# A graph-attention kernel with a larger ring of gathered tiles, smaller ALU layers, and extra TensorE products

## The chip, the cores and the metric

The kernel runs on one core of one Trainium2 chip. The metric is the device time of one execution in microseconds (us), the median of several runs. The profiles were taken from single executions of the same program.

## The reference

6250 nodes of 512 features and 100000 edges, sorted by their destination. First a layer of attention over the graph, then a small feed-forward "ALU" that reads a few features of each node. Cut to what matters:

```python
xn = layernorm(x)                                   # (6250, 512)
q, k, v = xn @ Wq + bq, xn @ Wk + bk, xn @ Wv + bv  # 8 heads of 64
logits = (q[rows] / 8 * k[cols]).sum(-1) + edge_attr          # (100000, 8)
att = segment_softmax(logits, rows)
y = segment_sum(att * v[cols], rows)
x = x + y @ Wo + bo
z = layernorm(x)
# ALU: 16-way decodes of z give four digits; two pipelines (add, sub)
# of three 160x160 layers with relu, on two positions of a node
out = x + z
out[:, 128:161] += one_hot(results), carry          # for active nodes
```

## The kernel before

**Two stages.** The first (0 to about 660 us of the span) sorts the edges on VectorE and, beside that, computes layer norm, K and V of all nodes on TensorE and writes them to DRAM as a table kv_d of 6250 rows of 1024 numbers (K and V side by side). The main stage follows: 49 blocks of 128 nodes (one node per partition). A block has a fixed number of edge slots, from 34 down to 8 (CAP), 804 in all; block b is cut into parts of at most 12 slots.

**A part.** Two slots share a tile kvt of [128, 2, 1024] float32 (8 KB in each partition), from a pool kvp of 11 buffers, the ring. For each slot GpSimd issues an indirect DMA (`gather`, L110) that fetches 128 rows of kv_d. It also fetches, some blocks ahead, the edges' records (rec), keys (kg) and node rows (xg), all in one queue in program order. The part is then worked on like this:

- `dots`: VectorE multiplies K by q in place (L814) and sums over each head (L815). So after L814 the K half of the tile holds the products k*q.
- `softmax`: VectorE takes the maximum and subtracts it, ScalarE takes the exponential (L752) and copies the weights into the PSUM tile pp (L756). pp has 256 columns, two halves used in turn.
- `sums`, called after the first dots of the next part (the list `waiting`): VectorE sums the weights (L767), VectorE multiplies the V half of most tiles by the weights in pp (L825), ScalarE does so for the last one or two full tiles (L823), and TensorE adds all slots up into the PSUM tile p_y by matmuls with the identity (L1105). The last of these matmuls on a tile frees it for the ring.
- `part_end`, a generator: VectorE adds p_y to y (L1064, L1068), divides (L790); `attend_out` transposes y on TensorE (L833), ScalarE copies it (L836), TensorE multiplies it by Wo (L842), VectorE adds x (L846).
- `project` (a generator too) makes q of the next block: transposes of xg (L803), a ScalarE copy (L805), the product with Wq (L809).

A float32 matmul of 512 columns stands in the trace as two passes.

**The ALU.** Four blocks form a group (the last are smaller). `alu` is a generator over the whole group's 512 nodes: TK = 512 nodes are taken at once through a first layer (L906, five matmuls, relu by ScalarE at L908 into h1), a second (L919, relu at L921 into h2) and a third (L926, copied by VectorE to yf at L929). All of them use the PSUM tag "mm", which has two buffers. The generator yields a kind ("P", "E" or "D") for the next step.

**Order.** All engines run in the order in which the program is written (`manual_schedule`). `pump(kinds)`, called once per tile before its `dots`, moves every generator in `going` one step, and the ALU one step if its kind is in `kinds` (`alu_steps`); at the end of a part up to four "P" steps are taken. So each engine has one fixed queue, in which a waiting instruction holds up all behind it.

SBUF holds, beside the ring, h1 and h2 (10 KB in each partition each), yf and fT (2 KB each in eight partitions), x1 and others.

Of the kernel before, what the change touches and what calls it, by code (L numbers as in the profile page):

```python
# [10 lines left out]
F32 = mybir.dt.float32  # L11
I32 = mybir.dt.int32
BF16 = mybir.dt.bfloat16
AF = mybir.ActivationFunctionType
# [6 lines left out]
P = 128  # L21
# [5 lines left out]
LOM = (1 << LOB) - 1  # L27
ROW = 9
GB = 4
TK = 512  # L30
LA = 6


# [10 lines left out]
def gnn_ffn_kernel(  # L44
# [3 lines left out]
    nc = tc.nc  # L48
    N, D = x.shape
    E = src.shape[0]  # L50
    H = edge_attr.shape[1]
# [22 lines left out]
    def ctile(shape, name, dt=F32, pool=const):  # L74
        return pool.tile(shape, dt, tag=name, name=name)
# [33 lines left out]
    def gather(dst_t, table, idx):  # L109
        nc.gpsimd.indirect_dma_start(  # L110
            out=dst_t, out_offset=None, in_=table,
            in_offset=bass.IndirectOffsetOnAxis(ap=idx, axis=0))
# [4 lines left out]
    wq = ctile([P, KC, D], "wq", pool=ow)  # L117
# [17 lines left out]
    NC4 = 4  # L135
# [87 lines left out]
    def fetch_keys(b):  # L223
        C = CAP[ORDER[b]]
        t, nbuf = ("0", 1) if b == 0 else ("", LA + 3)
        kg = pre.tile([P, C + 1], F32, tag="kg" + t, name="kg", bufs=nbuf)
        gather(kg, words, pos_i[:, ORDER[b]:ORDER[b] + 1])
        st[b] = dict(kg=kg)
# [18 lines left out]
    def fetch_recs(n, last):  # L247

        while fetched[0] < n and fetched[1] is not None and fetched[1][0] <= last:
            b, s = fetched[1]  # L250
            gather(st[b]["rec"][:, s, :], rec_d, st[b]["eid"][:, s:s + 1])
            fetched[:] = fetched[0] + 1, next(wanted, None)
# [5 lines left out]
    with tc.tile_pool(name="sort", bufs=1, side="right") as sp, \  # L258
# [75 lines left out]
        def zeros(shape, name):  # L334
            t = ctile(shape, name, pool=ow)
            nc.gpsimd.memset(t, 0.0)
            return t

        w0 = zeros([8, (NC4 + 1) * P], "w0")
        w2 = zeros([P, NC4 + 1, 2 * NC4], "w2")  # L340
# [388 lines left out]

    main = dict(reuse_waits="tile")  # L730
    ap_ = ctx.enter_context(tc.tile_pool(name="ap", bufs=2, **main))
    kvp = ctx.enter_context(tc.tile_pool(name="kvp", bufs=11, **main))
    o2 = ctx.enter_context(tc.tile_pool(name="o2", bufs=1, **main))
    ops = ctx.enter_context(tc.tile_pool(name="ops", bufs=2, space=PSUM, **main))

    turn_ = [0, 0]
    assert CG * H <= P
    pp = ops.tile([P, 2 * P], F32, tag="pp", name="pp", bufs=1)

    def softmax(lg, rec, m0):  # L740

# [57 lines left out]
    def project(xg, s_):  # L799

        pt = ops.tile([P, KC, P], F32, tag="tr", name="tr", bufs=1)
        for c in range(KC):
            nc.tensor.transpose(pt[:, c, :], xg[:, D + c * P:D + (c + 1) * P], ident)  # L803
        xT = o2.tile([P, KC, P], F32, tag="xT", name="xT", bufs=2)
        nc.scalar.copy(xT, pt)  # L805
        yield
        q = s_["q"] = ops.tile([P, D], F32, tag="q", name="q")
        for c in range(KC):
            nc.tensor.matmul(q, xT[:, c, :], wq[:, c, :], start=(c == 0), stop=False)  # L809
        nc.tensor.matmul(q, ones3, bq3, start=False, stop=True)  # L810

    def dots(kvt, n, q, dot, s):
        k = kvt[:, :n, :D]
        nc.vector.tensor_tensor(k, k, q[:, None, :].to_broadcast([P, n, D]), op=OP.mult)  # L814
        nc.vector.tensor_reduce(  # L815
            dot[:, s:s + n, :], k.rearrange("p s (h d) -> p s h d", h=H), AX.X, OP.add)
# [34 lines left out]
    def alu(x1, mv, n):  # L851
# [43 lines left out]
        fT = o2.tile([8, GB * P], F32, tag="fT", name="fT")  # L895
        nc.vector.tensor_copy(fT[:, :ntok], pf[:8, :ntok])  # L896


        yf = o2.tile([8, GB * P], F32, tag="yf", name="yf")
        for t0 in range(0, ntok, TK):  # L900
            t1 = min(t0 + TK, ntok)
            nt = t1 - t0
            h1 = o2.tile([P, NC4 + 1, TK], F32, tag="h1", name="h1")
            for c in range(NC4 + 1):
                pm = ops.tile([P, D], F32, tag="mm", name="pm3")
                nc.tensor.matmul(pm[:, :nt], w0[:, c * P:(c + 1) * P], fT[:, t0:t1],  # L906
                                 start=True, stop=True)
                nc.scalar.activation(h1[:, c, :nt], pm[:, :nt], AF.Relu,  # L908
                                     bias=b0[:, c:c + 1], scale=1.0)
                yield "P"  # L910
            h2 = o2.tile([P, NC4 + 1, TK], F32, tag="h2", name="h2")
            for c in range(NC4 + 1):
                if c < NC4:
                    terms = [(w1mm[c // 2], c), (w1lm[c], NC4)]
                else:
                    terms = [(w1ml[k], k) for k in range(NC4)] + [(w1ll, NC4)]
                pm = ops.tile([P, D], F32, tag="mm", name="pm4")
                for i, (w, k) in enumerate(terms):
                    nc.tensor.matmul(pm[:, :nt], w, h1[:, k, :nt],  # L919
                                     start=(i == 0), stop=(i == len(terms) - 1))  # L920
                nc.scalar.activation(h2[:, c, :nt], pm[:, :nt], AF.Relu,  # L921
                                     bias=b1[:, c:c + 1], scale=1.0)
                yield "P"
            p3 = ops.tile([P, D], F32, tag="mm", name="p3")[:8]
            for c in range(NC4 + 1):
                nc.tensor.matmul(p3[:, :nt], w2[:, c, :], h2[:, c, :nt],  # L926
                                 start=(c == 0), stop=(c == NC4))
            yield "D"
            nc.vector.tensor_copy(yf[:, t0:t1], p3[:, :nt])  # L929
# [51 lines left out]
    def fetch_nodes(b):  # L981
        if b - 4 in ends:
            run(ends.pop(b - 4))
        xg = ap_.tile([P, 2 * D], F32, tag="xg", name="xg", bufs=4)
        gather(xg, xx_d, nid[:, b:b + 1])
        st[b]["xg"] = xg
# [10 lines left out]
    kind = ["P"]  # L997
# [6 lines left out]
    def pump(kinds="", n=1):  # L1004

        last[1] += 1
        for g in list(going):
            if next(g, True):
                if g in going:
                    going.remove(g)  # L1010
        alu_steps(kinds, n)
        if stores and stores[0][0] + last[0] <= last[1]:
            store()

    def alu_steps(kinds, n):

        while alus and n > 0 and kind[0] in kinds:
            kind[0] = next(alus[0], None)
            if kind[0] is None:
                alus.pop(0)  # L1020
                kind[0] = "P"
            n -= 1

    def run(g):

# [87 lines left out]
    for b in range(NB):  # L1113
        C = CAP[ORDER[b]]
        s_ = st[b]
        rec, q = s_["rec"], s_["q"]
        parts = -(-C // PART)
        m = None
        for i in range(parts):
            s0, s1 = C * i // parts, C * (i + 1) // parts  # L1120
            n_ = s1 - s0
            dot = ap_.tile([P, n_, H], F32, tag="dot", name="dot", bufs=2)
            kvs = []
            for s in range(s0, s1, 2):
                n = min(2, s1 - s)
                kvt = kvp.tile([P, 2, 2 * D], F32, tag="kv", name="kv")
                for j in range(n):
                    gather(kvt[:, j, :], kv_d, rec[:, s + j, 0:1].bitcast(I32))
                kvs.append((kvt, n, s - s0))
                done = sum(SLOTS[:b]) + s + n  # L1130
                if done > HOLD:
                    last[0] = 1000
                fetch_recs(FIRST + (TOTAL - FIRST) * done // (TOTAL - LAST), b + LA)
                if s == s0 and i == 0:
                    if b + LA + 2 < NB:
                        fetch_keys(b + LA + 2)
                    if b + 1 < NB:
                        fetch_nodes(b + 1)
                if s == s0 + 2 and i == 0 and b + 1 < NB:
                    pj = project(st[b + 1]["xg"], st[b + 1])  # L1140
                    going.insert(0, pj)


                k = len(kvs) - 1
                pump("" if k < 2 else "D" if s + 2 >= s1 else "DE" if k == 2 else "DEP")
                dots(kvt, n, q, dot, s - s0)
                if s == s0:
                    for f in waiting:
                        f()
                    waiting.clear()  # L1150
                if s == s0 + 2 and i == parts - 1 and b + LA + 2 < NB:
                    read_keys(b + LA + 2)
            m, cor, p_ps = softmax(dot, rec[:, s0:s1], m)
            waiting.append(partial(sums, b, i, parts, dot, cor, p_ps, kvs, n_))
            alu_steps("P", min(4, len(kvs) - 1))
        if b + 1 < NB:
            run(pj)
# [150 lines left out]
```

## Time and profile before

| | |
|---|---|
| median of 14 runs | 3276.85 us (3251.86 to 3310.4) |
| the profiled execution, time | 3249.39 us |
| its span | 3247.6 us |
| mean granted TensorE clock | 0.801 |
| TensorE busy in the span | 2062.2 us (64%) |
| VectorE busy | 2004.7 us (62%) |
| ScalarE busy | 880.9 us (27%) |
| GpSimd busy | 1708.6 us (53%) |
| in the main stage, 660 to 3123 us: TensorE, VectorE, ScalarE, GpSimd busy | 1540, 1662, 638, 1504 us |
| granted clock, share of the DMA engines in it | 0.79, 0.57 |

How to read it: PE is TensorE, PEld its weight loads, DVE VectorE, ACT ScalarE, POOL GpSimd. A group's row gives the line, the engine, the operation, what it writes and reads, the count, then busy us and mean ns of one, then the idle time of the engine just before them and what ended most of it. The ends of matmuls are modelled. "issue" is a wait that the profile shows no cause for; "remote" and "an unknown queue" are waits whose end it cannot name. GpSimd's gathers take about 0.95 us each and are 0.30 us apart at the closest, and that gap is not counted as busy.

### The profile page before, as it was taken

The page shows a single profiled execution, that of the slowest core. Times are in us where ns is not written, and L with a number is a line of the kernel's source. Part 1 is how long each engine was busy: PE and PEld are TensorE (multiplying, and loading weights), DVE is VectorE, ACT ScalarE, POOL GpSimd, SP SyncE. Part 2 cuts the span into 40 slices and gives each one's busy share as a digit, 9 for nine tenths or more (in the row PEclk, how much of TensorE's full clock was granted, in tenths as well). Part 3 has the DMA queues.
Part 4 walks back from the last instruction along what each step waited for, and adds up shares of the span by engine and source line. Part 5 has one row for each costly group of instructions (what it writes and reads, how often), then busy time and mean ns, then how long its engine had stood idle before and what let it go on. Part 6 is the DMA issues. An engine that isn't in the chain of part 4 may idle for free. (4 is left out here: it accounts for less than half of the span.)

```text
span 3247.6 us, 20109 instructions
## 1 busy us (share of the span) xinstructions
PE 2062.2 (64%) x4853; PEld 889.9 (27%) x4853; DVE 2004.7 (62%) x3502; ACT 880.9 (27%) x2656; POOL 1708.6 (53%) x1860
## 2 busy tenths in 40 slices
PE   7887318743647645657476676757646748467686
PEld 3443103311212222222232232323222323123233
DVE  9887000075747655666686668768576756676772
ACT  6443003121113212222132222323213223122332
POOL 2010770165666565556655666666576555656630
PEclk9999658866868877878778888888877878788797
DMA  8443113366545455555655656665566555646630
GB/s 271 172 154 114 30 17 124 133 211 211 177 151 196 150 188 163 172 168 190 204 171 179 196 185 200 196 201 182 165 209 195 167 179 173 192 151 204 206 117 17
DMA packets 193964, 542.30 MB, mean 167 GB/s; under 512 B 51831, under 2 KB 53174, under 8 KB 193841
## 3 DMA queue, kind: packets, MB, share of 16 engines
q0 software_dynamic: 154416, 464.27, 44.9%
q1 hardware_dynamic: 39425, 76.67, 6.7%
q8 instruction: 42, 0.69, 0.1%
q14 instruction: 81, 0.66, 0.1%
HBM read 472.60 MB, written 68.22 MB: 167 GB/s over the span
## 5 line engine op out<-in xcount | busy, mean ns | idle before, releaser
L110 POOL DMA_INDIRECT kv<-kv_d,rec x804 | 760.4, 946 | 734.6 <-PE p_y L1105 300.8
L1105 PE MATMUL p_y<-kv,ident 128*128 128x512 f32 x1608 | 830.9, 673 | 351.2 <-issue 141.5
L110 POOL DMA_INDIRECT rec<-rec_d,eid x804 | 763.6, 950 | 245.1 <-issue 237.2
L814 DVE TENSOR_TENSOR kv<-kv,q 128x1024 f32<-128x1024 f32 (+1 forms) x425 | 490.2, 1153 | 199.1 <-DMA kv<-kv_d,rec 123.2
L1105 PEld LDWEIGHTS p_y<-kv,ident 128*128 128x128 f32 x1608 | 337.5, 216 | 819.1 <-issue 532.4
L815 DVE TENSOR_REDUCE dot<-kv 128x16 f32<-128x1024 f32 (+1 forms) x425 | 493.9, 1162 | 65.3 <-ACT kv L823 31.0
L809 PE MATMUL q<-wq,xT 128*128 128x512 f32 x392 | 212.9, 693 | 296.8 <-issue 203.9
L823 ACT ACTIVATE kv<-kv,dot 128x64 f32<-128x64 f32 x1568 | 387.3, 336 | 33.2 <-issue 32.2
L825 DVE TENSOR_TENSOR kv<-kv,pp 128x1024 f32<-128x1024 f32 (+1 forms) x327 | 352.7, 1137 | 0.0
L842 PE MATMUL pm<-wo,yT 128*128 128x512 f32 x392 | 215.4, 701 | 187.9 <-issue 101.4
L467 PE MATMUL pm<-wv,xnT 128*128 128x512 f32 (+1 forms) x392 | 190.2, 621 | 17.6 <-issue 17.6
L805 ACT COPY xT<-tr 128x512 f32<-128x512 f32 x49 | 28.7, 585 | 619.6 <-remote 328.6
L809 PEld LDWEIGHTS q<-wq,xT 128*128 128x128 f32 x392 | 82.6, 222 | 398.2 <-issue 301.4
L467 PE MATMUL pm<-wk,xnT 128*128 128x512 f32 (+1 forms) x392 | 187.7, 620 | 0.0
L842 PEld LDWEIGHTS pm<-wo,yT 128*128 128x128 f32 x392 | 86.2, 229 | 299.3 <-issue 205.9
L767 DVE TENSOR_REDUCE den<-dot 128x8 f32<-128x64 f32 (+6 forms) x91 | 24.8, 272 | 209.9 <-issue 114.4
L836 ACT COPY yT<-tr 128x512 f32<-128x512 f32 x49 | 28.6, 584 | 461.2 <-remote 248.4
L478 ACT COPY kvt<-pm 128x512 f32<-128x512 f32 (+1 forms) x98 | 57.1, 584 | 320.8 <-remote 132.3
L416 DVE RECIPROCAL rstd<-rstd 128x7 f32<-128x7 f32 (+4 forms) x9 | 1.7, 185 | 209.3 <-ACT rstd L412 160.1
L1068 DVE TENSOR_TENSOR y<-y,p_y 128x512 f32<-128x512 f32 x42 | 28.7, 682 | 158.0 <-remote 84.1
L906 PE MATMUL pm<-fT,w 8*128 8x512 f32 (+2 forms) x140 | 93.3, 793 | 47.2 <-DVE fT L896 19.6
L110 POOL DMA_INDIRECT xg<-xx_d,nid x49 | 46.2, 943 | 145.1 <-DMA xx_d<-xn 125.3
(258 smaller groups left out, 2119.0 us busy)
## 6 DMA issues: line engine op xcount, KB each, us to landing
kv_d<-kvt SPq DMA_DIRECT2D x48, 512.0 KB
rec<-rec_d,eid POOLq DMA_INDIRECT x804
kv<-kv_d,rec POOLq DMA_INDIRECT x804
xt<-in_x_dram SPq DMA_DIRECT2D x48, 256.0 KB
xx_d<-xt SPq DMA_DIRECT2D x48, 256.0 KB
xx_d<-xn SPq DMA_DIRECT2D x48, 256.0 KB
rec_d<-R SPq DMA_DIRECT2D x3, 882.0 KB
bt<-in_edge_attr_dram SPq DMA_DIRECT2D x3, 686.0 KB
```

The costliest lines, as they stand in the source:

```text
L110: nc.gpsimd.indirect_dma_start(out=dst_t, out_offset=None, in_=table, in_offset=bass.IndirectOffsetOnAxis(ap=idx, axis=0))
L467: nc.tensor.matmul(pm[:r], xnT[b][:, c, :r], wkv[nm_][:, c, :], start=(c == 0), stop=(i == 1 and c == KC - 1))
L478: nc.scalar.copy(kvt[:r, i * D:(i + 1) * D], pm[:r])
L805: nc.scalar.copy(xT, pt)
L809: nc.tensor.matmul(q, xT[:, c, :], wq[:, c, :], start=(c == 0), stop=False)
L814: nc.vector.tensor_tensor(k, k, q[:, None, :].to_broadcast([P, n, D]), op=OP.mult)
L815: nc.vector.tensor_reduce(dot[:, s:s + n, :], k.rearrange("p s (h d) -> p s h d", h=H), AX.X, OP.add)
L823: nc.scalar.mul(v[:, i, h], v[:, i, h], p[:, s + i, h:h + 1])
L825: nc.vector.tensor_tensor(v, v, p_ps[:, s:s + n, :, None].to_broadcast([P, n, H, DK]), op=OP.mult)
L842: nc.tensor.matmul(pm, yT[:, c, :], wo[:, c, :], start=(c == 0), stop=False)
L906: nc.tensor.matmul(pm[:, :nt], w0[:, c * P:(c + 1) * P], fT[:, t0:t1], start=True, stop=True)
L1105: nc.tensor.matmul(p_y, ident, kvt[:, j, D:], start=(done_ == 0), stop=(done_ == n_ - 1))
```

## The change

The ring kvp grows from 11 tiles to 13. Its memory comes from the ALU: TK falls from 512 to 256, so that a group of four blocks is done in two halves; h1 and h2 become one tile h of six chunks, in which the second layer writes over the first (its fifth output, which needs all of the first layer, is made first and goes to the sixth chunk); yf becomes the same tile as fT. A "P" step of the ALU now counts half in `alu_steps`, since a step has half the work.

[...] For each tile but the first of a part, two matmuls of 16 x 256 outputs are issued after its dots: 16 columns of the K half of the tile before it against 256 columns of wq. Nothing reads them. Since the K half is read after L814 has written it, these products wait for that.

```diff
-TK = 512
+TK = 256
...
-    kvp = ctx.enter_context(tc.tile_pool(name="kvp", bufs=11, **main))
+    kvp = ctx.enter_context(tc.tile_pool(name="kvp", bufs=13, **main))
...
-    pp = ops.tile([P, 2 * P], F32, tag="pp", name="pp", bufs=1)
+    pp = ops.tile([P, 4 * P], F32, tag="pp", name="pp", bufs=1)
+    idle = pp[:2 * H, 2 * P:]
...
-        yf = o2.tile([8, GB * P], F32, tag="yf", name="yf")
+        yf = fT
...
-            h1 = o2.tile([P, NC4 + 1, TK], F32, tag="h1", name="h1")
+            h = o2.tile([P, NC4 + 2, TK], F32, tag="h", name="h")
...
-                nc.scalar.activation(h1[:, c, :nt], pm[:, :nt], AF.Relu,
+                nc.scalar.activation(h[:, c, :nt], pm[:, :nt], AF.Relu,
...
-            h2 = o2.tile([P, NC4 + 1, TK], F32, tag="h2", name="h2")
-            for c in range(NC4 + 1):
+            at = [k if k < NC4 else NC4 + 1 for k in range(NC4 + 1)]
+            for c in [NC4] + list(range(NC4)):
...
-                nc.scalar.activation(h2[:, c, :nt], pm[:, :nt], AF.Relu,
+                nc.scalar.activation(h[:, at[c], :nt], pm[:, :nt], AF.Relu,
...
-                nc.tensor.matmul(p3[:, :nt], w2[:, c, :], h2[:, c, :nt],
+                nc.tensor.matmul(p3[:, :nt], w2[:, c, :], h[:, at[c], :nt],
...
         while alus and n > 0 and kind[0] in kinds:
+            n -= 0.5 if kind[0] == "P" else 1
             kind[0] = next(alus[0], None)
             if kind[0] is None:
                 alus.pop(0)
                 kind[0] = "P"
-            n -= 1
...
                 dots(kvt, n, q, dot, s - s0)
+
+                if s > s0:
+                    for c in range(2):
+                        nc.tensor.matmul(
+                            idle, kvs[-2][0][:, 0, :2 * H],
+                            wq[:, c, :2 * P], start=True, stop=True)
```

More of the change, by code (lines that the diff above doesn't have):

```diff
@@ L918, in alu @@
                 for i, (w, k) in enumerate(terms):
-                    nc.tensor.matmul(pm[:, :nt], w, h1[:, k, :nt],
+                    nc.tensor.matmul(pm[:, :nt], w, h[:, k, :nt],
                                      start=(i == 0), stop=(i == len(terms) - 1))
-                nc.scalar.activation(h2[:, c, :nt], pm[:, :nt], AF.Relu,
+                nc.scalar.activation(h[:, at[c], :nt], pm[:, :nt], AF.Relu,
                                      bias=b1[:, c:c + 1], scale=1.0)
```

## The prediction

> **What bounds the kernel now.** I read the page first, from its chain to the costliest groups, then the waits of VectorE and GpSimd in the main stage (660 to 3123 us of the span, between the first sums and the last gather), then a timeline and short windows.
>
> From the page, the chain that ended last and four groups:
>
> ```profile
> PE 17%; DVE 11%; issue 8%; another core or an unknown queue 6%; ACT 3%; DMA 1%; POOL 0%; POOLq 0%; DVEq 0%; ACTq 0%
> L110 POOL DMA_INDIRECT kv<-kv_d,rec x804 | 760.4, 946 | 734.6 <-PE p_y L1105 300.8
> L1105 PE MATMUL p_y<-kv,ident 128*128 128x512 f32 x1608 | 830.9, 673 | 351.2 <-issue 141.5
> L814 DVE TENSOR_TENSOR kv<-kv,q 128x1024 f32<-128x1024 f32 (+1 forms) x425 | 490.2, 1153 | 199.1 <-DMA kv<-kv_d,rec 123.2
> L809 PE MATMUL q<-wq,xT 128*128 128x512 f32 x392 | 212.9, 693 | 296.8 <-issue 203.9
> ```
>
> The tempting row is the first group: GpSimd stands 300.8 us until a sum (L1105) frees a tile of the ring, and a ring of 13 looks like the cure. But the chain contains no GpSimd. Its shares add up to 46% of the span (it can be followed back to 1777 us only); of those, TensorE's work is 17/46 = 37% and the time in which nothing visible runs ("issue" and "unknown queue") 14/46 = 30%.
>
> Whether earlier gathers would help is told by who waits for them. VectorE's waits in the main stage (us in all, times, longest):
>
> ```profile
> DVE den L767 <- issue: 114.4, 15, 24.5
> DVE y L1068 <- remote: 84.1, 9, 26.3
> DVE den L767 <- ACT dot L752: 62.9, 12, 25.3
> DVE kv L814 <- issue: 34.2, 4, 15.0
> DVE kv L814 <- DMA kv<-kv_d,rec: 14.8, 7, 3.9
> DVE kv L814 <- remote: 14.2, 1, 14.2
> ```
>
> VectorE works 1662 of 2463 us there. Before L814, the first instruction that needs a gathered tile, it idles for gathers at most 34.2 + 14.8 + 14.2 = 63 us. The other 740 us go to ScalarE's exponentials (L767 needs them) and to TensorE's results. The gathers already run ahead enough.
>
> What makes TensorE's results late shows in a timeline (start, duration, instruction, idle time before):
>
> ```profile
> 1803.43 0.60 PE L833 MATMUL tr<-ident,y 128*128 128x128 f32 x4
> 1825.68 0.59 ACT L836 COPY yT<-tr 128x512 f32<-128x512 f32 x1 [26.97 <-remote]
> 1824.49 0.94 POOL L110 DMA_INDIRECT kv<-kv_d,rec  x1 [3.16 <-remote]
> ```
>
> and in the DMA column of windows of 2 us (the columns: PE, PEld, DVE, ACT, POOL, clock, DMA share, GB/s):
>
> ```profile
> 1818.00:1820.00 2.00, 0.00 (x0) 0.00 (x0) 0.00 (x0) 0.00 (x0) 1.70 (x2) 0.50 0.70 211
> 1820.00:1822.00 2.00, 0.00 (x0) 0.00 (x0) 0.00 (x0) 0.00 (x0) 1.02 (x2) 0.50 0.88 301
> 1824.00:1826.00 2.00, 0.00 (x0) 0.00 (x0) 0.00 (x0) 0.32 (x1) 1.21 (x2) 0.50 0.00 0
> ```
>
> The four transposes of y are over at 1804 by the trace; the copy that waits for nothing but them starts at 1825.7. For 20 us TensorE and ScalarE stand still, VectorE for the last 16 of them, while gathers run, and the copy goes the moment the DMA share falls to 0.00, which happens because the ring is full and GpSimd stops. The same follows the p_y products at 2044 (yT at 2051.57, when the share is 0.00). So a part of TensorE's results is signalled late while gathers keep the DMA engines busy. [...]
>
> **The change, part by part.** Sums are against the profiled execution: 3249.4 us, span 3247.6; it is 27.5 us under the median of the runs shown, 3276.85.
>
> *Ring of 13.* GpSimd gets two tiles more room, each of two kv and two rec gathers at 0.95 + 0.30 us, so 10 us of lead. Best case: the 63 us that VectorE waits for gathers go. Worst case: a late result that is released only when the DMA engines fall quiet comes up to 10 us later; GpSimd has about 15 stops of over 8 us in the main stage, 150 us. I take 0, since the waits at L814 are small and the two effects oppose.
>
> *Layers of 256 nodes in place.* Eleven groups have 512 nodes; each relu of 512 (687 ns, L908 and L921) becomes two of 256 (473 ns, from the group of 256 in the tail): 2 x 473 - 687 = 259 ns, x 10 x 11 = 28 us more ScalarE, which is 26% busy in the main stage. TensorE's passes double in number at half length (in the tail two passes of 256 start within 0.43 us, as one of 512 does). One VectorE step more per group (the yf copy of the first half, 679 ns for 512 columns), with the second half's second matmul behind it, since "mm" has two buffers. A step "P" counts half, so the pace per call stays. Writing in place adds no wait: each relu that overwrites h[c] needs the PSUM of matmuls that have read it. Bounds 0 to +40 us, I take +20.
>
> *The products.* In the order of instructions of the built kernels there are 668 of them, 334 pairs: one per tile but the first of each part (425 - 91). A product is two passes of 256 columns; so a pair takes 4 x 0.215 = 0.86 us at the full clock, 1.72 at half, and 0.86/0.79 x 334 = 363 us at the main stage's mean clock of 0.79. TensorE idles 2463 - 1540 = 923 us there, which is the cover. But each pair is a fixed place in its queue, behind VectorE's product of the tile before (L814). Behind the pairs stand wo, q, the layers and the next part's sums. Behind transposes a pair runs while ScalarE copies (TensorE's pause there is 0.68 us, so 0.2 us sticks out); where TensorE works off a backlog, after each late result, all three to five pairs of the part are in the way. Bounds 0 (all covered) to +363; TensorE is 37% of the chain, and pairs beside a wait cost nothing, so a quarter: +90.
>
> *What the products do for the clock.* The mean passes are 673 (L1105), 693 (L809), 701 (L842) against 592 for the warm one, the median of L1105: 81 x 1608 + 101 x 392 + 109 x 392 ns = 213 us of slow clock, the most to gain. Where does the clock fall? Its changes stand on a grid of 3.4 us, and the window before decides:
>
> ```profile
> 1756.20:1759.60 3.40, 1.13 (x2) 0.30 (x2) 2.97 (x7) 3.40 (x16) 2.54 (x3) 1.00 0.56 163
> 1759.60:1763.00 3.40, 2.82 (x4) 1.28 (x5) 0.00 (x0) 1.11 (x4) 2.74 (x3) 0.50 0.56 175
> 2807.50:2810.90 3.40, 1.46 (x8) 0.66 (x6) 3.26 (x7) 0.00 (x0) 2.52 (x3) 1.00 0.55 162
> 2810.90:2814.30 3.40, 0.00 (x0) 0.00 (x0) 1.22 (x1) 0.00 (x0) 2.49 (x4) 1.00 0.83 289
> ```
>
> With 1.13 us of TensorE in a window the next is at 0.50; with 1.46 us the next is still at 1.00. A pair is 0.86 us, and VectorE reaches a new tile every 1.21 + 1.22 us of dots, with weighing 3.6: one pair per window as a rule, too little alone. It holds windows that have some 0.5 us of other work. And in the long pauses VectorE stands still too, so the pair's operand does not come. Bounds 0 to -213; a fifth: -40. [...]
>
> *A new wait.* The products write the unused half of the PSUM tile pp. In the built order the copy of the softmax weights into pp (L756, now L757) waits for TensorE in 91 of its instances; before, in none. So weighing a part now needs a signal from TensorE that its last pair is done. Queued behind that copy on ScalarE: cor, the copies of y, xT, yT, the relus and the weighing by ScalarE (L823); VectorE waits at den and at the weighing L825, and TensorE's sums for those. On time it costs nothing, as the last pair needs a tile two dots back. When signals are late (30% of the chain) it costs a wait like those before L767: 209.9 us in 31 waits, 6.8 us each. 91 x 0.30 x 6.8 = 186 us if none was blocked already, 0 if all were (xT and yT stand in the same ScalarE queue and wait for the same signals). I take +50, near the blocked side.
>
> Sum: 0 + 20 + 90 - 40 + 50 = +120; 3249.4 + 120 = 3369, and with the 27.5 us between this execution and the median 3397 us, some 3.7% slower.
>
> **The rivals.**
> *Faster (A).* The clock holds and the ring pays. Half of the 213 us was on the path and goes (-107), the 63 us of gather waits go, the pairs lie in pauses, and the layers cost 20: -150, so 3127 us. For it: 923 us of idle TensorE and the GpSimd row. Against: the windows of 3.4 us, and 63 us at L814 as the whole wait for gathers. It decides if the main stage's clock rises above about 0.9 and L767's waits do not grow.
> *No difference (B).* The pairs are all covered and hold no clock, the copy's wait is never last: 3277 us. Against it: 91 new waits in one queue with everything of ScalarE's.
> *Much slower (C).* More writes by TensorE while gathers run make more results late, and the copy at L757 waits in nearly each part: 91 x 6.8 = 619 us on top of 3277, 3896; half of that, 3587, is where it begins.
> That the change doesn't do what it says is excluded for the ring and the layers, but "keeps TensorE awake" is just what I doubt.
>
> **How the numbers follow.** Forecast (some per cent slower) 0.55, A 0.25, B 0.07, C 0.13. A measurement of this kernel can tell about 0.3% from no change, 10 us; B's time lies in that band for about 0.05, its rest falls to both sides. Faster 0.26, same 0.05, slower 0.69. The forecast's own ends: products at 0 give 3307, products at 200 and the copies at 130 give 3587. The range reaches down into A to 3200, at half of A's gain, and up to 3570 near C's start; it leaves out about 0.1 on each side.
>
> **What would show it.** Right: the products at 334 pairs with 0.86 to 1.7 us each; mean clock in the main stage under 0.87; ScalarE's L757 idle for TensorE; VectorE's waits before L767 above 210 us; GpSimd's wait on p_y shorter or equal with no gain in the span; idle before L814 still under 100 us. Wrong: a clock near 0.95 with L1105 at about 600 ns; VectorE's idle time in the main stage clearly under 800 us; or GpSimd busy without stops, which would mean that gathers were the limit after all.

## The result, and the profile after

The changed kernel takes 3619.86 us (median of 10 runs, 3593.65 to 3632.99) where the kernel before takes 3277.25 us (47 runs): ratio 1.1099 [1.1067, 1.1131], +343 us. The profiled execution took 3615.65 us, its span 3613.6 us, with a mean clock of 0.812 (0.801 before). The main stage, 665 to 3470 us, is 2805 us long instead of 2463: 342 of the span's 366 us were lost there, and VectorE works as long in it as before (1657 us, 1662 before).

From the page of the changed kernel, the chain and the groups that answer to those of before, with the new products and the copy of the softmax weights:

```profile
PE 43%; another core or an unknown queue 24%; DVE 15%; issue 12%; ACT 5%; POOL 1%; DMA 1%; ACTq 0%; POOLq 0%; SPq 0%; DVEq 0%
L110 POOL DMA_INDIRECT kv<-kv_d,rec x804 | 760.0, 945 | 1034.4 <-PE p_y L1107 598.8
L1107 PE MATMUL p_y<-kv,ident 128*128 128x512 f32 x1608 | 813.2, 664 | 400.6 <-DVE kv L826 269.5
L815 DVE TENSOR_TENSOR kv<-kv,q 128x1024 f32<-128x1024 f32 (+1 forms) x425 | 489.9, 1153 | 159.7 <-DMA kv<-kv_d,rec 105.6
L1152 PE MATMUL pp<-wq,kv 128*16 128x256 f32 x1336 | 337.2, 391 | 27.6 <-issue 13.9
L757 ACT COPY pp<-dot 128x64 f32<-128x64 f32 (+6 forms) x91 | 20.2, 221 | 568.6 <-remote 432.0
```

The ring is two tiles longer, and GpSimd stands still 300 us longer for a sum to free a tile (598.8 us against 300.8). The copy at L757 does 20.2 us of work, and ScalarE stands 568.6 us before it; before the change (L756) it stood there 2.9 us. What cannot be named now carries 24% of the chain, and this chain can be followed back over the whole span.

ScalarE's waits say the same by what ended them (us in all, times, longest):

```profile
ACT pp L757 <- remote: 432.0, 48, 31.7
ACT yT L837 <- remote: 256.4, 13, 28.0
ACT pp L757 <- PE pp L1152: 91.2, 17, 8.6
ACT xT L806 <- remote: 86.7, 5, 23.5
```

The copy of xT waited 328.6 us for "remote" before the change, so part of the 568.6 us was there already and only changed its place. VectorE's waits in the main stage (665 to 3470 us) show what is queued behind the copy:

```profile
DVE den L770 <- ACT cor L762: 133.1, 20, 29.7
DVE den L768 <- ACT dot L753: 114.1, 10, 20.8
DVE kv L826 <- ACT pp L757: 113.1, 16, 18.8
```

Before L770 and L826 (then L769 and L825) VectorE stood 1.7 and 0.0 us before the change. One such place in a timeline of the changed kernel (start, duration, instruction, idle time before), and below it the windows at its end (PE, PEld, DVE, ACT, POOL, clock, DMA share, GB/s):

```profile
1493.62 2.76 PE L1152 MATMUL pp<-wq,kv 128*16 128x256 f32 x12
1496.31 0.66 PE L834 MATMUL tr<-ident,y 128*128 128x128 f32 x4
1513.84 0.23 ACT L757 COPY pp<-dot 128x80 f32<-128x80 f32 x1 [20.91 <-remote]
```

```profile
1510.00:1512.00 2.00, 0.00 (x0) 0.00 (x0) 0.00 (x0) 0.00 (x0) 0.00 (x0) 0.50 0.70 252
1512.00:1514.00 2.00, 0.00 (x0) 0.00 (x0) 0.00 (x0) 0.16 (x1) 0.00 (x0) 0.50 0.01 2
```

By the trace the products are over at 1496.4; the copy that needs them starts 17 us later, when the DMA share falls from 0.70 to 0.01. It looks like the event of 1803 to 1825 us in the trace of before, now at the copy.

### The profile page after: what moved, and what is told of

Its sections match the earlier page's. It is cut to its first block, busy times and chain, and to the rows that moved or that the text cites. A ratio compares the mean times of both kernels' runs of the same rounds, so it can differ in the third digit from the quotient of the medians.

```text
span 3613.6 us, 23934 instructions
## 1 busy us (share of the span) xinstructions
PE 2432.7 (67%) x6695; PEld 1111.2 (31%) x6695; DVE 2010.6 (56%) x3513; ACT 903.8 (25%) x2766; POOL 1708.0 (47%) x1860
## 4 chain that ended last, share of the span: by engine, by line
PE 43%; another core or an unknown queue 24%; DVE 15%; issue 12%; ACT 5%; POOL 1%; DMA 1%; ACTq 0%; POOLq 0%; SPq 0%; DVEq 0%
PE p_y L1107 15%; PE pm L467 7%; PE pm L921 5%; PE pm L843 4%; PE pp L1152 3%; DVE kv L815 3%; PE pm L908 3%; DVE dot L816 3%; PE q L810 2%; DVE kv L826 2%; PE p L928 2%; ACT kv L824 1%; DVE key L143 1%; DVE key L144 1%
## 5 line engine op out<-in xcount | busy, mean ns | idle before, releaser
L110 POOL DMA_INDIRECT kv<-kv_d,rec x804 | 760.0, 945 | 1034.4 <-PE p_y L1107 598.8
L1107 PE MATMUL p_y<-kv,ident 128*128 128x512 f32 x1608 | 813.2, 664 | 400.6 <-DVE kv L826 269.5
L1107 PEld LDWEIGHTS p_y<-kv,ident 128*128 128x128 f32 x1608 | 337.7, 215 | 841.3 <-issue 510.8
L815 DVE TENSOR_TENSOR kv<-kv,q 128x1024 f32<-128x1024 f32 (+1 forms) x425 | 489.9, 1153 | 159.7 <-DMA kv<-kv_d,rec 105.6
L826 DVE TENSOR_TENSOR kv<-kv,pp 128x1024 f32<-128x1024 f32 (+1 forms) x327 | 352.9, 1138 | 180.6 <-ACT pp L757 114.3
L1152 PE MATMUL pp<-wq,kv 128*16 128x256 f32 x1336 | 337.2, 391 | 27.6 <-issue 13.9
L843 PE MATMUL pm<-wo,yT 128*128 128x512 f32 x392 | 205.6, 673 | 159.5 <-ACT yT L837 151.5
L810 PE MATMUL q<-wq,xT 128*128 128x512 f32 x392 | 193.1, 638 | 46.0 <-issue 40.9
L908 PE MATMUL pm<-fT,w 8*128 8x256 f32 (+1 forms) x250 | 112.2, 576 | 125.4 <-ACT h L910 43.6
L1152 PEld LDWEIGHTS pp<-wq,kv 128*16 128x16 f32 x1336 | 113.7, 98 | 225.3 <-issue 96.1
L843 PEld LDWEIGHTS pm<-wo,yT 128*128 128x128 f32 x392 | 81.8, 217 | 266.7 <-ACT yT L837 159.0
L757 ACT COPY pp<-dot 128x64 f32<-128x64 f32 (+6 forms) x91 | 20.2, 221 | 568.6 <-remote 432.0
L768 DVE TENSOR_REDUCE den<-dot 128x8 f32<-128x64 f32 (+6 forms) x91 | 24.8, 272 | 220.9 <-ACT dot L753 115.2
L923 ACT ACTIVATE h<-pm,b 128x256 f32<-128x256 f32 (+1 forms) x125 | 58.3, 469 | 354.6 <-PE pm L921 195.3
L770 DVE TENSOR_TENSOR den<-den,cor 128x8 f32<-128x8 f32 x42 | 7.0, 166 | 235.0 <-ACT cor L762 133.1
L478 ACT COPY kvt<-pm 128x512 f32<-128x512 f32 (+1 forms) x98 | 57.1, 584 | 317.7 <-remote 132.2
```

The source lines that it names most:

```text
L110: nc.gpsimd.indirect_dma_start(out=dst_t, out_offset=None, in_=table, in_offset=bass.IndirectOffsetOnAxis(ap=idx, axis=0))
L826: nc.vector.tensor_tensor(v, v, p_ps[:, s:s + n, :, None].to_broadcast([P, n, H, DK]), op=OP.mult)
L843: nc.tensor.matmul(pm, yT[:, c, :], wo[:, c, :], start=(c == 0), stop=False)
L1107: nc.tensor.matmul(p_y, ident, kvt[:, j, D:], start=(done_ == 0), stop=(done_ == n_ - 1))
L1152: nc.tensor.matmul(idle, kvs[-2][0][:, 0, :2 * H], wq[:, c, :2 * P], start=True, stop=True)
```

## The experiments

The runs fell on six chips, and this turned out to matter most: on one (runs e1 to e4) the kernel before takes 3273 us, as in the first result; on the five others it takes 2637 to 2642 us. I call them the late chip and the ordinary chips. Whether the late chip is the very one of the first result is not recorded; its times and traces agree with it. Each run is compared with the kernel before on its own chip.

| kernel | late chip: us, against before | ordinary chips: us, against before |
|---|---|---|
| before | 3272.61 | 2637.45 to 2641.5 |
| layers of 256 alone | not run | 2660.83 to 2665.82; 1.0083 to 1.0093 in four comparisons |
| ring 13 + layers (no products) | 3394.62; 1.0414 [1.0299, 1.0529] | 2631.74; 0.9973 [0.9964, 0.9983] |
| the same, one product per part | 3432.35; 1.0516 [1.0397, 1.0635] | 2661.58; 1.0081 [1.0061, 1.0100] |
| products alone (ring 11, layers of 512) | not run | 2682.47; 1.0165 [1.0148, 1.0182] |
| the change | 3619.86 (first result) | 2698.06; 1.0224 [1.0201, 1.0247] |
| weights in SBUF, ring 13 + layers, no products | 3317.79; 1.0173 [1.0057, 1.0290] | not run |
| the same with all products | 3454.58; 1.0579 [1.0460, 1.0698] | not run |
| weights in SBUF, else as before | not run | 2754.23; 1.0443 [1.0423, 1.0463] |
| before with ring 9 | not run | 2685.1 and 2690.8; 1.0177 and 1.0187 |
| ring 12, layers of 512 in place | not run | 2626.72 and 2627.03; 0.9963 [0.9951, 0.9975], 0.9953 [0.9936, 0.9969] |

**On the late chip: what the products cost.** The first theory (W) was that the new wait of the copy makes most of the 343 us; its rivals, the products' own time in TensorE's queue (Q) and the ring or the layers (R).

e1 takes the products out:

```diff
-    pp = ops.tile([P, 4 * P], F32, tag="pp", name="pp", bufs=1)
-    idle = pp[:2 * H, 2 * P:]
+    pp = ops.tile([P, 2 * P], F32, tag="pp", name="pp", bufs=1)
...
-                if s > s0:
-                    for c in range(2):
-                        nc.tensor.matmul(
-                            idle, kvs[-2][0][:, 0, :2 * H],
-                            wq[:, c, :2 * P], start=True, stop=True)
```

> The changed kernel without its 668 products: ring of 13 tiles and layers of 256 stay. Theory W (most of the 343 us is the wait of the copy into pp, L757, for TensorE's last product, signalled late) and theory Q (most of it is the time of the products themselves in TensorE's queue) both expect the kernel before plus the layers' estimated 20 us and a ring that costs nothing: 3250 to 3320 us. Theory R (the ring of 13 prolongs the stretches in which gathers keep TensorE's signals back, or the split layers stretch the queue) expects 3400 us or more. ScalarE's idle time before the copy should fall from 568.6 to under 250 us by W and Q, and stay over 400 us by R.

Measured 3394.62 us, against W and Q, and 5 us under what R asked: the ring and the layers alone lose 122 us here (98 to 173 by the interval). The copy's wait is gone (2.9 us), which R did not expect. ScalarE's late waits went to other places:

```profile
ACT xT L805 <- remote: 341.0, 12, 43.1
ACT h L922 <- remote: 149.7, 20, 19.1
```

e2 and e3 put the softmax weights into an SBUF tile, so that the copy cannot wait for TensorE, without products (e2) and with all of them in a PSUM tile of their own (e3):

```diff
-    pp = ops.tile([P, 4 * P], F32, tag="pp", name="pp", bufs=1)
-    idle = pp[:2 * H, 2 * P:]
+    pp = o2.tile([P, 2 * P], F32, tag="pp", name="pp", bufs=1)
+    idle = ops.tile([P, 2 * P], F32, tag="idle", name="idle", bufs=1)[:2 * H]
```

> A control for the next run: no products, and the softmax weights are copied into an SBUF tile instead of PSUM (the copy stays, VectorE's weighing reads SBUF). All theories expect it near the run without products, within 60 us: the weighing takes 1138 ns from PSUM, 327 times, and an SBUF operand may change that by some 10% (37 us of VectorE).

> All 668 products stay, but in a PSUM tile of their own; the softmax weights are copied into SBUF, so the copy waits for TensorE in none of its 91 instances. Read against the control without products. Theory W: the loss goes, 0 to 120 us over the control, ScalarE's idle time before the copy under 250 us. Theory Q: the products still stand in TensorE's queue, 250 us or more over the control, and TensorE's waits for products show up before yT, h and the exponentials. A gain over the control of more than 30 us would say that the products do keep the clock, and that only their place in pp costs.

Measured 3317.79 and 3454.58 us. The control missed its expectation: it is 77 us under e1. Against it the products cost 137 us without any wait of the copy (2.9 us before it), where W allowed 120 at most and Q asked for 250: neither holds. With the copy's tile shared they cost 3620 - 3395 = 225 us, so sharing it is worth about 88 us of that. This is an estimate: the 3620 us may come from another chip, and the two pairs differ in where the weights lie.

e4 keeps all 91 waits and a seventh of the products:

```diff
-                if s > s0:
-                    for c in range(2):
+                if s > s0 and s + 2 >= s1:
+                    for c in range(1):
```

> One product in each part, at its last tile, in place of two at every tile but the first: 91 instead of 668, so a seventh of TensorE's extra time, and the same 91 waits of the copy into pp. Theory W: still slow, 3480 to 3620 us, with over 400 us of ScalarE's idle time before the copy. Theory Q: 3300 to 3360 us (the run without products plus 91/668 of the 343 us, 47 us).

Measured 3432.35 us, below W's range and above Q's. Q's range was written before e1 was known; over e1 the 91 products cost 38 us, near the 47 us of its working. Of ScalarE's waits before the copy, 212.7 us in all, the two largest:

```profile
ACT pp L757 <- PE pp L1152: 91.7, 22, 7.2
ACT pp L757 <- remote: 71.2, 13, 10.8
```

The copy can wait in as many places as in the changed kernel, idles 213 us, and the whole costs 38 us: ScalarE's 568.6 us of idle time before the copy were not 568.6 us of cost.

**On an ordinary chip: the parts alone.** e5 undoes the ring and the products, e6 puts the products alone into the kernel before, e7 and e8 change one thing in the kernel before, the place of the weights and the ring:

```diff
-    pp = ops.tile([P, 2 * P], F32, tag="pp", name="pp", bufs=1)
+    pp = o2.tile([P, 2 * P], F32, tag="pp", name="pp", bufs=1)
...
-    kvp = ctx.enter_context(tc.tile_pool(name="kvp", bufs=11, **main))
+    kvp = ctx.enter_context(tc.tile_pool(name="kvp", bufs=9, **main))
```

> The layers of 256 nodes in place alone: ring of 11, no products. The run without products was 122 us slower than before, and this run splits that. Theory R (the two more tiles let gathers keep the DMA engines busy longer, so TensorE's signals come later): 3285 to 3330 us, the estimated 20 us of the layers and no more. Theory L (the layers: twice the passes, and twice the number of results that ScalarE must wait for, each possibly signalled late): 3360 to 3420 us, with ScalarE's waits before the relus (h) well above the 235 us that the kernel before has in its listed rows.

> The kernel before (ring of 11, layers of 512) with the 668 products in pp alone. With the ring and the layers in place the products cost 225 us (3620 against 3395). If parts of the change add up, 3272 + 225 = about 3500 us; ScalarE's idle time before the copy into pp over 400 us as in the changed kernel. If products cost more because the ring or the layers already keep the queue full, under 3430 us. The forecast's own sum for them (90 for the products, 50 for the wait, minus 40 for the clock) gives 3370 us.

> The kernel before with the softmax weights copied into SBUF instead of PSUM. In the pair without products this took 77 us off (3395 to 3318), while GpSimd's gathers took 1005 instead of 948 ns each. Theory S (slower gathers leave TensorE's signals earlier): the same here, 3170 to 3230 us, with gathers of about 1000 ns. If the gain belonged to the ring of 13 or to the layers alone: 3250 to 3300 us.

> The kernel before with a ring of 9 tiles in place of 11. Theory R (a longer ring keeps signals back longer): faster or equal, 3180 to 3280 us, GpSimd's stops on p_y longer in sum, ScalarE's and VectorE's waits for TensorE shorter. Theory L leaves the ring no such part: 3280 to 3400 us, with waits of VectorE for gathers (L814) that grow from 123 us.

Measured 2662.82, 2682.47, 2754.23 and 2685.10 us beside 2637.81 us for the kernel before. All four expectations were written for 3273 us and miss; what is read is the differences: layers +25, products +45, SBUF +116, a ring of 9 +47 us. In none of the four traces is any wait of any engine put down to "remote".

The SBUF run has the other sign than e2 had on the late chip, though e2 is another kernel (ring of 13, layers of 256), so chip and kernel are not told apart here. Its row of gathers, and VectorE's wait for them:

```profile
L110 POOL DMA_INDIRECT kv<-kv_d,rec x804 | 827.4, 1029 | 259.1 <-issue 198.1
```

```profile
DVE kv L814 <- DMA kv<-kv_d,rec: 340.2, 162, 16.5
```

With the weights in SBUF, so that both operands of VectorE's weighing lie there, GpSimd's gathers take 1029 ns instead of 947, and VectorE waits 340 us for them instead of 182 (the kernel before on another ordinary chip, below). Between e2 and e1 it was 1005 against 948 ns. How the one lengthens the other is not shown.

**The whole change on an ordinary chip.** e9 is the changed kernel, e10 the layers alone, e11 the kernel of e1, on one chip:

> The changed kernel itself, beside its parts on the same chip. In the last four runs the kernel before took 2638 us, and none of their waits for TensorE is put down to 'remote'; the layers alone cost 25 us and the products alone 45 us. Theory S (signals that come late multiply every wait for TensorE, and only the chip of the first result has them): on a chip where before takes about 2638 us the parts add up to 2690 to 2730 us, 2 to 3.5% slower; where before takes about 3270 us it is 3590 to 3635 us again. Theory A (the change costs what it costs wherever it runs): 343 us over before in either case, 2980 us where before takes 2638.

> Ring of 11, layers of 256 in place, no products. Where before takes 2638 us: 2663 us as before. Where it takes 3270 us: by theory R (ring) 3285 to 3330 us, by theory L (twice as many signals of the layers come late) 3360 to 3420 us.

> Ring of 13, layers of 256, no products; the difference to the run with ring 11 is the ring alone. Where before takes 2638 us: 9 tiles cost 47 us against 11 there, because VectorE waited 239 us for gathers, so two more tiles should gain 10 to 40 us: 2620 to 2655 us. Where it takes 3270 us: 3395 us as measured.

Measured 2698.06, 2660.83 and 2631.74 us beside 2638.84: the number is the one that theory S gave, and A falls. S's reason, that late signals multiply every wait, is not shown by it. The change costs 59 us there: layers +22, ring of 13 minus 29, products +66. From the page and ScalarE's waits of e9, the same kernel that has 568.6 us before the copy on the late chip:

```profile
PE 54%; DVE 22%; issue 10%; POOL 8%; DMA 4%; ACT 2%; DVEq 0%; POOLq 0%; SPq 0%; ACTq 0%
L110 POOL DMA_INDIRECT kv<-kv_d,rec x804 | 760.1, 945 | 288.2 <-issue 193.3
L1107 PE MATMUL p_y<-kv,ident 128*128 128x512 f32 x1608 | 770.3, 637 | 192.0 <-DVE kv L826 192.0
```

```profile
ACT pp L757 <- PE pp L1152: 177.6, 62, 6.0
```

"Remote" is gone from the chain and from every engine's waits; the copy waits 2.9 us at a time for products that are really not done, and 6.0 us at the most. The products do raise the clock: 0.915 over the span against 0.870 in e11, and a pass of L1107 takes 637 ns against 654. It does not pay. VectorE now waits for the copy (L826) and for the exponential queued behind it (L770), where e11 has no such rows:

```profile
DVE den L770 <- ACT cor L762: 48.1, 21, 6.0
DVE kv L826 <- ACT pp L757: 32.2, 19, 5.1
```

It gains 24 us at L815 (gathers, 74.5 to 50.2 us). Added up, these idle times make 56 of the 66 us; that is an account, not a proof.

**The products without most of their time, and a better version.** e13 is the kernel of e4, e12 is meant to beat both: layers in place but 512 wide, a ring of 12 in the room, no products.

```diff
-    kvp = ctx.enter_context(tc.tile_pool(name="kvp", bufs=11, **main))
+    kvp = ctx.enter_context(tc.tile_pool(name="kvp", bufs=12, **main))
...
-            h1 = o2.tile([P, NC4 + 1, TK], F32, tag="h1", name="h1")
+            h = o2.tile([P, NC4 + 2, TK], F32, tag="h", name="h")
```

> A version meant to beat both: layers in place but still 512 wide (so none of the layers' added steps), a ring of 12 in the room that this frees, no products. Where before takes 2638 us: 9 tiles cost 47 us and 13 gained 29 us, so 12 should gain 15 to 25 us: 2613 to 2625 us. Where before takes 3270 us: by theory R (ring) slower by 30 to 60 us, by theory L (layers) no slower than 3290 us.

> One product per part (91), all 91 waits of the copy into pp. Where before takes 2638 us the 668 products cost 66 us (2632 to 2698). If most of that is the copy's wait: 2670 to 2700 us, ScalarE's idle time before the copy still near the 178 us of the changed kernel. If it is the products' time in TensorE's queue: 2632 + 91/668 x 66 = 2641 us, up to 2650. Where before takes 3270 us: 3432 us as measured.

e13: 2661.58 us on a chip where before takes 2637.45. It is 30 us over e11 (on another ordinary chip) with a seventh of the products, between both expectations: ScalarE still waits 103.0 us before the copy for them, VectorE 21.9 us at L826 and 21.4 at L770. So about 30 of the 66 us come with 91 waits and 91 products, and the other 36 with the remaining products, of which the copy's longer wait (177.6 us) is a part. e12: 2626.72 us, 2 us above its expectation and 0.4% faster than before: 11 us, where the ring of 13 with split layers gained 7. It was run on ordinary chips only.

**The kernel before on an ordinary chip, and what stayed open.** e14 is the kernel before; e15 to e18 were to split ring and layers on the late chip, but ran on ordinary ones.

> The kernel before, unchanged, for its trace. Where it takes 2638 us: no wait for TensorE put down to 'remote', the copies of xT and yT together idle for about 600 us as in the other runs there but off the chain, GpSimd's stops on p_y under 60 us in sum (300.8 in the first profile), mean clock 0.87. Where it takes 3270 us: as in the first profile.

> Ring of 11, layers of 256 in place, no products. Where before takes 2638 us: 2661 us. Where it takes 3270 us: theory R (the ring makes the 122 us): 3285 to 3330 us; theory L (the layers make it): 3360 to 3420 us.

> The kernel before with a ring of 9. Where before takes 2638 us: 2685 us. Where it takes 3270 us: theory R 3180 to 3280 us, theory L 3280 to 3400 us.

> Ring of 12, layers of 512 in place, no products. Where before takes about 2640 us: 2622 to 2632 us. Where it takes about 3270 us: theory R (the ring makes the 122 us) 3310 to 3370 us, theory L (the split layers make it) no more than 3290 us.

> Ring of 11, layers of 256 in place, no products. Where before takes about 2640 us: 2661 to 2666 us. Where it takes about 3270 us: theory R 3285 to 3330 us, theory L 3360 to 3420 us.

e14: 2640.52 us, with the copies of xT and yT idle for 621 us, GpSimd's stops on p_y 22.9 us and a clock of 0.871, as expected. e15 to e18 repeat the differences: 2665.82 (+24), 2690.80 (+49), 2627.03 (-12) and 2661.25 us (+23). From the waits and a timeline of e14:

```profile
DVE kv L814 <- DMA kv<-kv_d,rec: 182.2, 101, 15.3
ACT yT L836 <- PE tr L833: 219.5, 34, 19.1
```

```profile
1715.25 0.66 PE L833 MATMUL tr<-ident,y 128*128 128x128 f32 x4
1717.71 0.58 ACT L836 COPY yT<-tr 128x512 f32<-128x512 f32 x1
```

The transposes of y start at 1715.25 and the copy runs at 1717.71, 2.5 us later; on the late chip this took 22 us. Nor are the 2.5 us TensorE's: ScalarE works on the exponential (L752) and the copy into pp (L756) just before. There is no wait for "remote" on any engine (ScalarE alone has 844 us in 53 waits in the first profile). Yet the DMA engines are busier: a share of 0.70 in the main stage (510 to 2515 us), 0.57 in the first profile. What bounds this chip is another thing: VectorE waits 182 us for gathers, which is why a longer ring pays here.

"Remote" is a label, and the traces of the late chip hold fewer records of signals (13244 against 38100 for the same program, so "issue" and the shares of the chain are rough there). So the delay was also counted without it, for the 98 copies of xT and yT: from the end of the transposes by the trace, or of ScalarE's instruction before if that is later, to the start of the copy. In the first profile 22 copies are over 8 us late, the longest 34.9 us, 488 us in all. In the 14 traces from ordinary chips none is over 0.1 us late. The products that wait for these copies (L809, L842) start within 0.1 us in the first profile too: what ScalarE gives TensorE is on time, what TensorE gives ScalarE is not.

Which of the ring and the layers makes the 122 us on the late chip is not settled. ScalarE's waits for "remote" before the relus grew from 48.5 us (7) in the first profile to 161.5 us (22) in e1, those before xT and yT fell from 577 to 521.5 us; that points to the layers, but idle time is no price. Nor is it settled why this chip signals late, or whether recording has a part in it: every time on record comes with a recorded span.

## Why the prediction was right or wrong

*Direction.* Right: slower on the chip forecast for (+343 us), and on the ordinary ones (+59 us). *Size.* Wrong: +120 was forecast, and +343 lies above the range.

*The layers (+20, bounds 0 to 40).* The number was right wherever they could be measured alone: +22 to +25 us on four ordinary chips. Where that time goes was not looked into.

*The ring (0, bounds -63 to +150).* On ordinary chips minus 29 us, for the reason that was given for its best case: VectorE's waits for gathers at L814 fall, from 109.5 us with ring 11 (e10) to 74.5 with 13 (e11), on the same chip. On the late chip ring and layers together cost 122 us where the sum had 20. The reading "the gathers already run ahead enough" was right for that trace, but not of the kernel: on an ordinary chip VectorE waits 182.2 us for gathers (e14).

*The products (+90), the copy's wait (+50) and the clock (-40), together +100.* Measured +225 on the late chip and +66 on the ordinary ones. The mechanisms named are among those that the runs show. The clock term, -40, holds in TensorE's time, if not on the path: the passes of L1107 fell from 673 to 664 ns, of L810 from 693 to 638 and of L843 from 701 to 673, 9 x 1608 + 55 x 392 + 28 x 392 ns = 47 us. The main stage's clock went from 0.79 to 0.80, and the span's from 0.870 to 0.915 between e11 and e9, so the small term that the windows gave was near. Two windows were few, though. In the whole first profile none of the 86 windows at full clock with under 1.4 us of TensorE was followed by full clock, 19 of 28 with 1.4 to 2.1 us were, and 449 of 453 with more. So the window of 1.46 us lies at the edge. The wait was read as 88 us and the products' own part as 137 us, both above what was taken and inside their bounds.

*The step that failed* is the pricing of a late result, in two places. First, the sum charged the ring nothing, the layers what their own instructions add, and the products "a quarter" of their time; only the copy's term counted waits (91 x 0.30 x 6.8 = 186 us), and it was taken near its blocked side. On the late chip the ring and the layers cost 122 us where the sum had 20, the products 137 us where it had 50 (90, less 40 for the clock), and the copy's wait about 88 us where it had 50: each 1.8 to 6 times its price. In the traces late results stand in their place: ScalarE's waits for "remote" went from 53 (844 us) to 61 (910 us) with ring and layers and to 111 (1122 us) with the products. That every further result for which an engine waits is another chance to be late fits these counts, but is argued: 66 us more of such waits stand beside a loss of 122 us. Second, the range was made as if the worst case of each term excluded that of the others, although by this reading one cause drives them; rival C had it at 3587 us and up, with a chance of 0.13. C's reason was only partly right: the copy does wait in 77 of 91 instances, 568.6 us, close to its 619; but xT's copy idled 619.6 us before and 392.7 after, and taking the wait away gained about 88 us.

*The inference about the cause.* That TensorE's results come late holds. "While gathers keep the DMA engines busy", released when they fall quiet, was read from picked cases and does not. Of the 22 copies over 8 us late in the first profile, 6 start after a last microsecond with a DMA share under 0.05, and 14 after one with over 0.5. The latest of all, xT's copy at 1178.06 us, 34.9 us after its transposes, has this behind it (columns as above):

```profile
1177.10:1178.10 1.00, 0.00 (x0) 0.00 (x0) 0.00 (x0) 0.04 (x1) 0.69 (x2) 0.50 0.69 238
```

And in the first stage, which the prediction left out, six of the 98 copies of K and V (L478) wait for "remote", 132.3 us in all. All six start between 352 and 492 us, while the DMA engines are nearly quiet and GpSimd issues gathers of records one after another; of the other 92 none is over 3 us late. The window before one of them, then 100 us of the first profile and 84 us at the same place in e14:

```profile
353.30:375.00 21.70, 0.00 (x0) 0.00 (x0) 0.00 (x0) 0.04 (x1) 16.37 (x18) 0.50 0.12 4
400.00:500.00 100.00, 14.03 (x23) 5.40 (x23) 0.00 (x0) 6.50 (x14) 63.80 (x68) 0.53 0.11 22
400.00:484.00 84.00, 66.35 (x180) 30.08 (x178) 0.00 (x0) 19.10 (x33) 63.39 (x68) 0.92 0.35 108
```

With the same work of GpSimd beside it (64 and 63 us), TensorE is busy 14 of 100 us on the late chip and 66 of 84 us on the ordinary one. So in this stage the delays go with GpSimd's issuing and not with the load of the DMA engines, and on the late chip alone; what links the two is not shown. The stage loses 146 us by it or beside it: the first gather of K and V starts at 629.7 us, in e14 at 484.1.

*What was to show it.* As told: 334 pairs (1336 passes in 668 products), 1.01 us of TensorE each, a main clock under 0.87 (0.80), the copy idle for TensorE, waits before L768 above 210 us (220.9). Not as told: GpSimd's wait on p_y was to be shorter or equal and doubled to 598.8 us, since the sums that free tiles come later when all before them does.

## What to carry to other kernels

Filler work for TensorE should have a PSUM tile of its own: here a shared one made the softmax's copy wait for products that nobody reads, and on an ordinary chip the clock that they kept (0.870 to 0.915) was worth less than the queue and the wait (+66 us). A tile of its own was run only together with weights in SBUF (e3). An engine's idle time before one line is no price for that line; take the wait away and see what becomes late next (568.6 us of idle time, about 88 us of gain). And where a trace has many waits that it cannot name, run the kernel before on another chip before tuning for them: ring and layers, which together gain 7 us on an ordinary chip, cost 122 us on the late one, and the whole change costs 59 and 343 us.

## What the hardware showed that was not expected

One program took 3273 us on one chip and 2637 to 2642 us on five others, with the same instructions. VectorE's work was the same (2005 us against 2007 us busy); what differs in the traces is when TensorE's results are seen, up to 34.9 us after the trace's matmuls on the one and at most 0.1 us on the others, and 844 us of ScalarE's waits without a name against none. Putting 91 small copies into SBUF instead of PSUM changed the time by -77 us on the one chip (ring of 13, layers of 256) and by +116 us on another (the kernel before). In both the gathers became slower, by 57 and 82 ns each; why the late chip gained is not shown.
